# Layer 1's products with adj: from all 22 column blocks to the row block's own columns and a listed, gathered rest

## The chip, the cores and the metric

One core of a Trainium2 chip runs the whole program. The metric is the device time of one execution in microseconds (us). Five runs of the kernel before took 1628.26 to 1630.18 us, with a median of 1629.69 us. The engines are named as in the profile: PE (matmul; PEld loads its weights), DVE (vector), ACT (scalar), POOL (GpSimd) and SP (here only a queue that issues transfers).

## The reference, cut to what matters

A graph of N = 2708 nodes with D = 256 features; `adj` is a 2708 x 2708 matrix in which an off-diagonal element is non-zero with probability 0.00295, and the diagonal is full.

```python
# layer 0
x = _layernorm(x + relu(concat([x, adj @ x], axis=1) @ weight + bias))
# layer 1
R = adj + eye(N);  R = R / R.sum(-1)
Xf = Xa = x
for n in range(2):
    A = _top_p_attention(Xa, W1, W2, W3)   # softmax, cut to the top 0.9 of each row's mass
    Xf = R @ Xf
    Xa = A @ Xa
    Z = Z + Xf @ U1[n].T + Xa @ U2[n].T
x = _layernorm(x + layernorm(x + Z) * ln_g + ln_b)
```

So `adj` is multiplied three times: once in layer 0 and twice in layer 1 (`R @ Xf`, then R times that).

## The kernel before, in words

Everything is float32. The nodes are cut into NB = 22 blocks of 128 rows (the last has 20). The host passes `adj` already transposed and blocked: `adj_d[m, p, k, i]` is the element of row `m*128+i` and column `k*128+p`, so that `adj_d[m, :, k, :]` is directly the weight operand of a matmul. The order of the instructions on each engine's queue is the order of the source (a manual schedule); the semaphores are put in by the framework, and a tile of a pool waits until all readers of the tile that had its room are done.

Layer 0 (L265 to L293) goes over m. `adj_product` (L192) adds 22 products of 128 x 128 by 128 x 257 in PSUM. Its operand comes in two halves, tiles of the pool `adjp` with three rooms, loaded by SP one block ahead (`adj_load`, L187). Two more matmuls add x's own share (L275), then DVE and ACT do the bias, the relu and the layernorm (L282 to L290), and PE turns x1's previous block (L257) and every fourth time projects queries and keys (L242, L247).

Layer 1's first attention step (L537 to L576): logits (L305), top-p by extraction (`extract1`, `finish1`), then for each block t a loop over six groups g: PE transposes four blocks of the masked weights (`turn`, L326), ACT copies them out of PSUM (L329), PE multiplies the group before (`products`, L341). `u1_project` (L427) makes `v` = x U1[0] and `yf` = x U1[1]; `u1_add` (L435) adds row-sum-scaled yf to v. `step1_out` gives the second step its input, ya, its queries and keys, and writes `za` to DRAM.

Layer 1's second step (L766 to L828) goes over periods `per` from -1 to 22, each with six slots g. In a period DVE finishes the top-p search of block `per` (`round_dve` L647, `finish2` L664 to L703, some 105 instructions), ACT does half-rounds of block per+1 and exps of block per+2, PE multiplies block per-1 and computes the logits of per+2. Between these PE does the products with adj: `r_units(n)` (L480) takes n units, a unit being one product of 128 x 128 by 128 x 256 (L197, two matmul records each). A row block takes 22 units, and there are two passes: s = 0 with `yf`, whose result goes into `v` (L511), and s = 1 with `v`, whose result goes to the outputs (L515). The table `units` (L761) says how many units a period takes: 24 before period 0, 84 in period 0, 31 in each of periods 1 to 10 and 49 or 50 in each of 11 to 21. In all 968 units. At the start of each slot 0 the units come before `turn` and before the logits of block per+2, and DVE's `shift` (L610) of those logits comes before or inside its first round.

A block is finished when both its second R product and its attention have arrived (`arrive`, L518); up to two finished blocks at a time then go through `Final` (L708): two layernorms on DVE with their square roots on ACT, spread over the slots, and the store. `za` and `x1b` come back from DRAM for this (L505, L717).

At the end a count of flags (L830 to L837) decides whether `general_path` computes layer 1 again in a slower way; with these inputs it does not run.

Of the kernel before, what the change touches and what calls it, by code (L numbers as in the profile page):

```python
# [8 lines left out]
FP = mybir.dt.float32  # L9
I32 = mybir.dt.int32  # L10
# [9 lines left out]
P = 128  # L20
# [5 lines left out]
ROUNDS = 5  # L26
V0, VSPAN = 0.9375, 88.0
TIE_EPS = 1.5e-5
TOP_S = 0.8999


def chunks(N):
    return [(a, min(N, a + CH)) for a in range(0, N, CH)]
# [6 lines left out]
@with_exitstack  # L40
def gnn_two_layer_kernel(ctx: ExitStack, tc: tile.TileContext, N, xT_d, x_d, adj_d, w0_d, b0_d,
                         w1_d, w2_d, w3_d, u1_d, u2_d, g_d, b_d, out_d):

    nc = tc.nc
    D = x_d.shape[1]
    DA = w1_d.shape[1]
    NB = (N + P - 1) // P
    DC = D // P
    assert N % 2 == 0 and NB % 2 == 0 and N * 2.0 ** -15 < 0.09 and DC == 2 and DA == 64
    assert SEG * (NS - 1) + 8 <= N <= SEG * NS
    CHS = chunks(N)
    KH = NB // 2

    def rows(t):
        return min(P, N - t * P)

    const = ctx.enter_context(tc.tile_pool(name="const", bufs=1))
    dram = ctx.enter_context(tc.tile_pool(name="dram", bufs=1, space=DRAM))
    ctx.enter_context(tc.manual_schedule())

    c = Common()
    c.N, c.D, c.DA, c.NB, c.DC, c.KH, c.CHS, c.rows = N, D, DA, NB, DC, KH, CHS, rows
    c.adj_d, c.out_d = adj_d, out_d  # L80
    c.x1_d = dram.tile([N, D], FP, name="x1_d")
    c.x1b_d = dram.tile([N, D], FP, name="x1b_d")
    c.za_d = dram.tile([N, D], FP, name="za_d")
    c.spill = dram.tile([N, 2 * D], FP, name="spill")


    c.ident = const.tile([P, P], FP, name="ident")
    c.eps = const.tile([P, 1], FP, name="eps")
    c.w1 = const.tile([P, DC, DA], FP, name="w1")
    c.w3 = const.tile([P, DC, DA], FP, name="w3")  # L90
    c.w2 = const.tile([DA, DA], FP, name="w2")
    c.u1 = const.tile([P, DC, 2, D], FP, name="u1")
    c.u2 = const.tile([P, DC, 2, D], FP, name="u2")
    c.gb = const.tile([P, 2, D], FP, name="gb")
    c.rinv = const.tile([P, NB], FP, name="rinv")
    NF = 5 * NB
    flags = const.tile([P, NF], FP, name="flags")
    fint = const.tile([1, 1], I32, name="fint")

    fast = ExitStack()  # L100
    with fast:
        fast_path(fast, tc, c, flags, fint, xT_d, x_d, w0_d, b0_d, w1_d, w2_d, w3_d, u1_d, u2_d, g_d, b_d)
    again = nc.values_load(fint[0:1, 0:1], min_val=0, max_val=P * NF,
                           skip_runtime_bounds_check_because="a count of 0/1 flags")
    with tc.If(again > 0):
        with ExitStack() as gen:
            general_path(gen, tc, c)
# [17 lines left out]
def fast_path(ctx, tc, c, flags, fint, xT_d, x_d, w0_d, b0_d, w1_d, w2_d, w3_d, u1_d, u2_d, g_d, b_d):  # L125
# [2 lines left out]
    ident = c.ident  # L128
    adj_d, out_d, x1_d, za_d = c.adj_d, c.out_d, c.x1_d, c.za_d
    NW = SEG * NS  # L130

    big = ctx.enter_context(tc.tile_pool(name="big", bufs=1))
    adjp = ctx.enter_context(tc.tile_pool(name="adjp", bufs=3))
# [21 lines left out]

    w0 = es[0][:, :2 * DC * D].rearrange("p (c e) -> p c e", e=D)
    b0 = es[1][:, :D]
    nc.scalar.dma_start(out=w0, in_=w0_d.rearrange("(c p) e -> p c e", p=P))

    xT = big.tile([P, DC, N], FP, tag="Y", name="xT")  # L160
# [28 lines left out]
        nc.sync.dma_start(out=a, in_=adj_d[m, :, h * KH:(h + 1) * KH, :])  # L189
        adj_of.setdefault(m, []).append(a)  # L190

    def adj_product(acc, m, y, n, stop, k0=0, k1=NB):  # L192
        p = rows(m)
        halves = adj_of[m]
        for k in range(k0, k1):
            kw = rows(k)
            nc.tensor.matmul(acc[:p, :n], lhsT=halves[k // KH][:kw, k % KH, :p], rhs=y[:kw, k, :n],  # L197
                             start=k == 0, stop=stop and k == NB - 1)
        if k1 == NB:
            adj_of.pop(m)  # L200


    adj_load(0, 0)
# [19 lines left out]


    wqq = small.tile([P, DC, 2, DA], FP, tag="wqq", name="wqq", bufs=1)
    w1n = small.tile([DA, DC, P], FP, tag="w1n", name="w1n", bufs=1)
    for j in range(DC):
        tr = ps_tr()
        nc.tensor.transpose(tr[:DA, 0, :], c.w1[:, j, :], ident)
# [32 lines left out]
        qk_project(0, a, b, lambda j: x1T[:, j, a:b])  # L262

    CB = CH // P
    for m in range(NB):  # L265
        p = rows(m)
        xt = work.tile([P, D], FP, tag="in", name="xt", bufs=3)
        nc.scalar.dma_start(out=xt[:p], in_=x_d[m * P:m * P + p, :])
        acc = ps_acc()
        adj_product(acc, m, y0, D + 1, False)  # L270
        if m + 1 < NB:
            adj_load(m + 1, 0)
            adj_load(m + 1, 1)
        for j in range(DC):
            nc.tensor.matmul(acc[:p, :D], lhsT=xT[:, j, m * P:m * P + p], rhs=w0[:, j, :],  # L275
                             start=False, stop=j == DC - 1)
        if m:
            x1_transpose(m - 1)
        if m >= CB and m % CB == 0:
            x1_qk(m // CB - 1)  # L280
        h = work.tile([P, D], FP, tag="mid", name="h")
        nc.vector.tensor_add(h[:p], acc[:p, :D], b0[:p])  # L282
        nc.vector.scalar_tensor_tensor(h[:p], h[:p], 0.0, xt[:p], op0=ALU.max, op1=ALU.add)
        nc.vector.tensor_scalar(rinv[:p, m:m + 1], acc[:p, D:D + 1], 1.0, None, op0=ALU.add)
        mv, sd = ln_stats(nc, small, c.eps, h, p)
        nc.vector.reciprocal(rinv[:p, m:m + 1], rinv[:p, m:m + 1])
        ln_apply(nc, x1[:p, m, :], h, p, mv, sd)
        nc.sync.dma_start(out=x1_d[m * P:m * P + p, :], in_=x1[:p, m, :])
        xb = work.tile([P, D], FP, tag="x1b", name="xb")
        nc.vector.tensor_add(xb[:p], x1[:p, m, :], c.gb[:p, 1, :])  # L290
        nc.sync.dma_start(out=c.x1b_d[m * P:m * P + p, :], in_=xb[:p])
    x1_transpose(NB - 1)
    x1_qk(len(CHS) - 1)  # L293

# [128 lines left out]
    def u1_project(t):  # L423
        p = rows(t)
        pz = ps_acc()
        for j in range(DC):
            nc.tensor.matmul(pz[:p], lhsT=x1T[:, j, t * P:t * P + p],  # L427
                             rhs=c.u1[:, j].rearrange("p s e -> p (s e)"), start=j == 0, stop=j == DC - 1)
        nc.scalar.copy(v[:p, t, :], pz[:p, :D])
        nc.scalar.copy(yf[:p, t, :], pz[:p, D:])  # L430

    def u1_add(t):

# [34 lines left out]

    r_queue = [(s, m) for s in range(2) for m in range(NB)]
    r_now = []  # L470
    arrived, loads, held = {}, {}, {}
    later = []
    ready = []

    def run_later():
        now, later[:] = later[:], []
        for f in now:
            f()

    def r_units(n):  # L480
        for _ in range(n):
            s, m = r_queue[0]
            y = (yf, v)[s]
            if not r_now:
                r_now[:] = [ps_misc(), 0]
            acc, k = r_now
            if k in (0, KH) and len(r_queue) > 1:
                adj_load(r_queue[1][1], k // KH)
            adj_product(acc, m, y, D, True, k, k + 1)
            r_now[1] += 1  # L490
            if k + 1 == NB:
                r_now.clear()
                r_queue.pop(0)
                base = za_load(m) if s else None
                later.append(lambda s=s, m=m, acc=acc, base=base: r_out(s, m, acc, base))

# [11 lines left out]
    def r_out(s, m, acc, base):  # L508
        p = rows(m)
        if s == 0:  # L510
            nc.vector.scalar_tensor_tensor(v[:p, m, :], acc[:p, :D], rinv[:p, m:m + 1], v[:p, m, :],  # L511
                                           op0=ALU.mult, op1=ALU.add)
        else:
            tmp = work.tile([P, D], FP, tag="mid", name="rtmp")
            nc.vector.tensor_add(tmp[:p], acc[:p, :D], v[:p, m, :])  # L515
            arrive(m, base, tmp, rinv[:p, m:m + 1])
# [31 lines left out]
            ra = finish1(0)  # L548
    for t in range(n_u, NB):
        u1_project(t)  # L550
    adj_load(0, 0)
    adj_load(0, 1)
    ends = None
    for t in range(NB):
        acc = ps_acc()
# [2 lines left out]
        for g in range(NG):  # L558
# [5 lines left out]
            if part and g in (3, 4):  # L564
                part(g - 3)
            products(1)
            if g == 2:
                u1_add(t)
                if t + 3 < NB:
                    extract1(t + 3)  # L570
        ends = step1_out(t, acc, ra)
        ra = ra_next
    products(0)
    for f in ends:
        f()
        r_units(2)  # L576

# [178 lines left out]
    accs = {}  # L758


    units = {-1: 24, 0: 84}  # L761
    units.update({p: 31 for p in range(1, 11)})
    rest = NB * len(r_queue) - (r_now[1] if r_now else 0) - sum(units.values())
    units.update({11 + i: rest * (i + 1) // (NB - 11) - rest * i // (NB - 11) for i in range(NB - 11)})
    assert min(units.values()) > 20
    for per in range(-1, NB + 1):  # L766
        n_r = units.get(per, 0)
        b_act = blocks.get(per + 1) if per >= 0 else None
# [60 lines left out]

    nc.vector.tensor_scalar(flags[:, 2 * NB:3 * NB], bulk[:, 0, :], 1.0e30, None, op0=ALU.is_ge)  # L830
    nc.vector.tensor_scalar(flags[:, 3 * NB:4 * NB], bulk[:, 1, :], 0.0, None, op0=ALU.is_le)
    nc.vector.tensor_tensor(flags[:, 4 * NB:], bulk[:, 3, :], bulk[:, 2, :], op=ALU.is_ge)
    nc.vector.tensor_reduce(fcol, flags, AX.X, ALU.add)
    products(0)
    pf = ps_misc()
# [371 lines left out]
```

## Time and profile before

| | |
|---|---|
| median of 5 runs | 1629.69 us |
| the profiled execution | 1629.63 us |
| its span, first to last instruction | 1627.8 us |
| mean granted PE clock | 0.98 |
| busy: PE, DVE, ACT, POOL | 1557.5, 1125.0, 862.1, 1.5 us |
| layer 0 | 0 to 299 us |
| first step, until its last product | 299 to 777 us |
| second step, DVE's searches | 810 to 1595 us |
| the end | 1595 to 1628 us |

The span is measured from the first to the last instruction, and the execution's time lies 1.8 us above it. Idle time of an engine that is not the bottleneck costs nothing, so each stage has to be read by itself. Every transfer in this kernel is issued by the SP or the ACT queue; the table of queues has no row for POOL. The loads of adj's halves (704 KB each) are 132 issues, 66 blocks times two: a block for each of 22 row blocks in each of the three products.

### The profile page before, as it was taken

To read this page: it belongs to the slowest core of one execution; us is meant where nothing else is said; L and a number is where in the kernel's file an instruction comes from. 1 tells how busy PE (TensorE), PEld (TensorE's weight loads), DVE (VectorE), ACT (ScalarE), POOL (GpSimd) and SP (SyncE) were. 2 spreads that over 40 slices of the span, in tenths; PEclk is the share of its full clock that TensorE was granted. 3 is DMA by queue.
4 is the path that set the end of the run, shared out by engine and by line. 5 is a ranking of instruction groups with operands and counts; after the bars stand their busy time and mean duration, and the time that the engine had idled before them with its cause. 6 is when DMAs were issued, how large, how long until landed. Compare 5 with 4: busy or idle time off the path is not lost.

```text
span 1627.8 us, 20569 instructions
## 1 busy us (share of the span) xinstructions
PE 1557.5 (96%) x7008; PEld 1124.4 (69%) x7008; DVE 1125.0 (69%) x3950; ACT 862.1 (53%) x1470; POOL 1.5 (0%) x18
## 2 busy tenths in 40 slices
PE   8999999789999999999989999999999999999994
PEld 6877777336666666667666776777767777777862
DVE  1212212366777777771199999999988999999995
ACT  1000000345555555553348887887867777777710
POOL 0000000000000000000000000000000000000000
PEclk9999999899999999999999999999999999999997
DMA  5454454100000000000232222221232334333321
GB/s 195 150 160 144 142 162 148 44 0 4 7 7 7 7 7 10 8 7 13 88 107 66 73 78 75 69 79 61 81 96 85 116 108 137 104 109 119 115 77 34
DMA packets 50624, 126.16 MB, mean 78 GB/s; under 512 B 6042, under 2 KB 32334, under 8 KB 50510
## 3 DMA queue, kind: packets, MB, share of 16 engines
q1 hardware_dynamic: 44784, 119.87, 23.0%
q10 hardware_dynamic: 5726, 4.89, 1.1%
q8 instruction: 57, 0.93, 0.2%
q14 instruction: 57, 0.47, 0.1%
HBM read 111.01 MB, written 13.73 MB: 77 GB/s over the span
## 4 chain that ended last, share of the span: by engine, by line
PE 62%; DVE 33%; DMA 2%; issue 1%; ACT 1%; SPq 0%; DVEq 0%; ACTq 0%
PE acc L341 19%; PE acc L197 13%; PE misc L197 9%; DVE w L647 6%; PE lg L305 6%; DVE w L695 5%; PE tr L326 5%; DVE e L698 3%; DVE cand L669 3%; DVE w L664 3%; PE misc L459 3%; PE acc L427 2%; DVE spare L356 2%; DVE srt L354 2%; PE acc L275 1%
## 5 line engine op out<-in xcount | busy, mean ns | idle before, releaser
L329 ACT COPY wT<-tr 128x512 f32<-128x512 f32 (+2 forms) x264 | 136.0, 515 | 315.8 <-PE tr L326 312.8
L197 PE MATMUL misc<-yf,adj_t 128*128 128x256 f32 (+1 forms) x968 | 237.8, 393 | 5.5 <-DVE v L511 5.5
L341 PE MATMUL acc<-ya,wT 128*128 128x256 f32 (+1 forms) x968 | 242.6, 390 | 0.0
L341 PE MATMUL acc<-x,wT 128*128 128x256 f32 (+1 forms) x968 | 240.6, 387 | 0.0
L197 PE MATMUL misc<-v,adj_t 128*128 128x256 f32 (+1 forms) x968 | 228.6, 386 | 0.0
L341 PEld LDWEIGHTS acc<-x,wT 128*128 128x128 f32 (+1 forms) x968 | 169.1, 185 | 80.9 <-issue 46.4
L197 PEld LDWEIGHTS misc<-yf,adj_t 128*128 128x128 f32 (+1 forms) x968 | 175.0, 189 | 67.8 <-issue 37.1
L197 PE MATMUL acc<-y,adj_t 128*128 128x257 f32 (+1 forms) x968 | 218.7, 382 | 0.0
L341 PEld LDWEIGHTS acc<-ya,wT 128*128 128x128 f32 (+1 forms) x968 | 176.7, 187 | 52.6 <-ACT wT L329 14.5
L197 PEld LDWEIGHTS misc<-v,adj_t 128*128 128x128 f32 (+1 forms) x968 | 173.7, 186 | 49.9 <-issue 22.9
L197 PEld LDWEIGHTS acc<-y,adj_t 128*128 128x128 f32 (+1 forms) x968 | 175.7, 185 | 40.0 <-issue 11.5
L326 PE MATMUL tr<-ident,e 128*128 128x128 f32 (+1 forms) x968 | 151.4, 275 | 21.8 <-DVE e L698 21.8
L630 ACT ACTIVATE w<-e,st 128x2708 f32<-128x2708 f32 (+1 forms) x63 | 166.6, 2644 | 0.6 <-ACT e L613 0.6
L632 ACT ACTIVATE w<-e,st 128x2708 f32<-128x2708 f32 (+1 forms) x63 | 166.3, 2639 | 0.0
L305 PE MATMUL lg<-k,q 64*128 64x512 f32 (+3 forms) x528 | 151.8, 603 | 13.7 <-ACT e L312 13.7
L326 PEld LDWEIGHTS tr<-ident,e 128*128 128x128 f32 (+1 forms) x968 | 115.4, 140 | 67.8 <-issue 47.8
L347 DVE MAX8 cand<-e 128x8 f32<-128x170 f32 (+1 forms) x352 | 89.6, 321 | 80.2 <-ACT e L312 80.2
L647 DVE SCALAR_TENSOR_TENSOR w<-e,st 128x2720 f32<-128x2720 f32 (+1 forms) x47 | 143.4, 3051 | 1.7
L282 DVE TENSOR_TENSOR h<-acc,e 128x256 f32<-128x256 f32 (+1 forms) x22 | 9.3, 424 | 185.8 <-PE acc L275 185.8
L258 ACT COPY x1T<-tr 128x256 f32<-128x256 f32 (+1 forms) x22 | 8.0, 364 | 201.3 <-PE tr L257 201.3
L695 DVE MATCH_REPLACE8 w<-eq,w 128x178 f32<-128x178 f32 (+1 forms) x352 | 110.7, 327 | 0.0
L669 DVE MAX8 cand<-w 128x8 f32<-128x170 f32 (+1 forms) x352 | 87.3, 320 | 0.8
(153 smaller groups left out, 1581.7 us busy)
## 6 DMA issues: line engine op xcount, KB each, us to landing
adj_t<-in_adj SPq DMA_DIRECT2D x132, 704.0 KB, 4.2
base<-za_d SPq DMA_DIRECT2D x41, 128.0 KB, 3.3
xt<-in_x ACTq DMA_DIRECT2D x21, 128.0 KB, 2.1
x_d<-x SPq DMA_DIRECT2D x21, 128.0 KB, 1.7
x1b_d<-xb SPq DMA_DIRECT2D x21, 128.0 KB, 2.1
za_d<-za SPq DMA_DIRECT2D x21, 128.0 KB, 1.7
x1b<-x1b_d SPq DMA_DIRECT2D x21, 128.0 KB, 4.9
out<-o SPq DMA_DIRECT2D x21, 128.0 KB, 1.7
```

What stands on the lines that cost most here:

```text
L197: nc.tensor.matmul(acc[:p, :n], lhsT=halves[k // KH][:kw, k % KH, :p], rhs=y[:kw, k, :n], start=k == 0, stop=stop and k == NB - 1)
L305: nc.tensor.matmul(lg[:p, h, :b - a], lhsT=q[o, t * P:t * P + p], rhs=keys[s][o, i, :b - a], start=True, stop=True)
L326: nc.tensor.transpose(tr[:kw, k % 4, :p], e[:p, k * P:k * P + kw], ident[:p, :p])
L329: nc.scalar.copy(wT[:, :full, :p], tr[:, :full, :p])
L341: nc.tensor.matmul(acc[:p, :D], lhsT=wT[:kw, k % 4, :p], rhs=y[:kw, k, :], start=k == 0, stop=k == NB - 1)
L347: nc.vector.max(dst[:p, i * 8:(i + 1) * 8], src[:p, i * step:i * step + w])
L459: nc.tensor.matmul(pz[:p], lhsT=xaT[:, j, :p], rhs=c.u2[:, j].rearrange("p s e -> p (s e)"), start=j == 0, stop=j == DC - 1)
L630: nc.scalar.activation(scr[:b.p, :N], e, AF.Relu, bias=b.nz, scale=b.sq, accum_out=b.relu)
L632: nc.scalar.activation(scr[:b.p, :N], e, AF.Sign, bias=b.nz, scale=b.sq, accum_out=b.sign)
L647: nc.vector.scalar_tensor_tensor(w[:b.p, :, :SEG], e3(b.t)[:b.p], b.d, e3(b.t)[:b.p], op0=ALU.is_ge, op1=ALU.mult, accum_out=b.m)
L669: nc.vector.max(cv[:p, i, :], w[:p, i, :SEG])
L695: nc.vector.match_replace(w[:p, i, :], eq[:p, i * 8:(i + 1) * 8], w[:p, i, :], 0.0)
```

## The change

Layer 1's two R passes no longer multiply all 22 column blocks. Three things are new.

*Lists.* In layer 0, while the halves of adj's row block m are in SBUF, DVE reduces each `[128, 11, 128]` half over i to "has this column an element among the 128 rows" (`name_columns`) and writes a name, a number that grows with nothing but position, for each such column outside the block's own. `Lists` turns the names of three column blocks at a time onto one partition (PE, ACT), takes the largest 160 of the 384 names by 20 rounds of max and match_replace (DVE), raises a flag if one is left, and makes row numbers of them. The first list covers m < 16; its rounds run beside blocks 16 to 21. The second covers the other six; its rounds run in the first ten blocks of the first step, two in each. POOL writes the numbers to DRAM and reads them back as `ix`, 126 x 9 numbers for each m (7 segments of 162, the last two of each being empty).

*adj, gathered.* In the first step, in slot 3 of block t, POOL issues nine indirect transfers that gather 126 rows of 512 bytes each out of adj_d (`adj_gather`), and rebases ix by one small POOL instruction. Two blocks later SP stores the tile to DRAM (`adj_store`).

*The products.* `r_load(s, m)` loads the gathered adj of m, its own diagonal block, and by nine more indirect transfers on POOL (126 rows of 1 KB) the matching rows of yf or v, which are therefore also stored to DRAM. The matching rows go into `yg`, two buffers in turn, in the room that yf had. A row block takes CC + 1 = 10 units instead of 22, and `r_load` of m+1 is issued when m starts. `units` becomes 20 per period: s = 0 in periods 0 to 10, none in -1 and 11, s = 1 in 12 to 22. The six units among `ends` before the second step are gone too, as are the R passes' `adj_load`s. `u1_add` runs two blocks at a time in the first 11 blocks instead of one in each of 22.

```diff
-    def adj_product(acc, m, y, n, stop, k0=0, k1=NB):
+    def adj_product(acc, m, y, n, stop):
...
+    def name_columns(m):
+        for h in range(2):
+            nc.vector.tensor_reduce(some[:, h * KH:(h + 1) * KH], adj_of[m][h], AX.X, ALU.max,
+                                    apply_absolute_value=True)
+        nc.vector.tensor_scalar(some, some, 0.0, None, op0=ALU.not_equal)
+        for a, b, o in ((0, m, 0), (m + 1, NB, -1)):
+            if a < b:
+                nc.vector.scalar_tensor_tensor(names[:, m, a + o:b + o], ramp[:, a:b], -float(m * P * NB),
+                                               some[:, a:b], op0=ALU.add, op1=ALU.mult)
+    class Lists:
...
+        def turn(self):
...
+            for j in range(3):
+                nc.tensor.transpose(tr[:n, j, :], parts[:, :, j], ident)
+            nc.scalar.copy(self.row[:n].rearrange("q (j p) -> q j p", j=3), tr[:n, :3, :])
+            nc.vector.memset(self.top[:n, CAP:], 0.0)
+        def take(self, i0, i1):
+            n = self.n
+            for i in range(i0, i1):
+                t8 = self.top[:n, 8 * i:8 * i + 8]
+                nc.vector.max(t8, self.row[:n])
+                nc.vector.match_replace(self.row[:n], t8, self.row[:n], 0.0)
+        def end(self):
...
+            nc.gpsimd.dma_start(out=flat.rearrange("(r k) -> r k", k=CPAD), in_=self.int[:n])
+            nc.gpsimd.dma_start(out=ix[:CW, a:b, :], in_=c.list_d[a:b].rearrange("m p c -> p m c"))
+    def adj_gather(m):
+        a = adjp.tile([P, KH, P], FP, tag="adj", name="adj_t")
+        for i in range(CC):
+            nc.gpsimd.indirect_dma_start(out=a[:CW, i, :], out_offset=None, in_=adj_rows,
+                                         in_offset=bass.IndirectOffsetOnAxis(ap=ix[:CW, m, i:i + 1], axis=0))
+        nc.gpsimd.tensor_scalar(ix[:CW, m, :], ix[:CW, m, :], m * P * NB, P * NB - 1, op0=ALU.subtract, op1=ALU.min)
+        staged[m] = a
+    def adj_store(m):
+        nc.sync.dma_start(out=c.adjc_d[m], in_=staged.pop(m)[:CW, :CC, :].rearrange("p c i -> p (c i)"))
...
+        name_columns(m)
         adj_product(acc, m, y0, D + 1, False)
...
+        if m == ML:
+            lists.turn()
...
+        if m >= ML:
+            i = m - ML
+            lists.take(CAP // 8 * i // (NB - ML), CAP // 8 * (i + 1) // (NB - ML))
+    lists.end()
...
+        nc.sync.dma_start(out=c.yf_d[:p, t, :], in_=yf[:p, t, :])
...
+    def r_load(s, m):
+        a = adjp.tile([P, KH, P], FP, tag="adj", name="adj_t")
+        nc.sync.dma_start(out=a[:CW, :CC, :].rearrange("p c i -> p (c i)"), in_=c.adjc_d[m])
+        nc.sync.dma_start(out=a[:rows(m), CC, :], in_=adj_d[m, :rows(m), m, :])
+        y = yg[:, m % 2]
+        rows_d = (c.yf_d, c.v_d)[s].rearrange("p k d -> (p k) d")
+        for i in range(CC):
+            nc.gpsimd.indirect_dma_start(out=y[:CW, i, :], out_offset=None, in_=rows_d,
+                                         in_offset=bass.IndirectOffsetOnAxis(ap=ix[:CW, m, i:i + 1], axis=0))
+        if s == 0:
+            nc.sync.dma_start(out=y[:rows(m), CC, :], in_=c.yf_d[:rows(m), m, :])
+        r_in[s, m] = a, y
...
             if not r_now:
                 r_now[:] = [ps_misc(), 0]
+                if m + 1 < NB:
+                    r_load(s, m + 1)
             acc, k = r_now
-            if k in (0, KH) and len(r_queue) > 1:
-                adj_load(r_queue[1][1], k // KH)
-            adj_product(acc, m, y, D, True, k, k + 1)
+            a, y = r_in[s, m]
+            kw = CW if k < CC else p
+            rhs = v[:p, m, :] if s and k == CC else y[:kw, k, :]
+            nc.tensor.matmul(acc[:p, :D], lhsT=a[:kw, k, :p], rhs=rhs, start=k == 0, stop=k == CC)
...
+            nc.sync.dma_start(out=c.v_d[:p, m, :], in_=v[:p, m, :])
+            if m == NB - 1:
+                r_load(1, 0)
...
             products(1)
+            if g == 0 and t > 1:
+                adj_store(t - 2)
             if g == 2:
-                u1_add(t)
+                for k in range(2 * t, min(NB, 2 * t + 2)):
+                    u1_add(k)
...
+                if t < 10:
+                    lists.take(2 * t, 2 * t + 2)
+                if t == 9:
+                    lists.end()
+            if g == 3:
+                adj_gather(t)
...
+    for m in sorted(staged):
+        adj_store(m)
+    yg = big.tile([P, 2, CC + 1, D], FP, tag="Y", name="yg")
+    r_load(0, 0)
     for f in ends:
         f()
-        r_units(2)
...
-    units = {-1: 24, 0: 84}
-    units.update({p: 31 for p in range(1, 11)})
...
+    each = NB * (CC + 1)
+    units = {p: each * (p + 1) // 11 - each * p // 11 for p in range(11)}
+    units.update({p: each * (p - 11) // 11 - each * (p - 12) // 11 for p in range(12, 23)})
```

## The prediction

> **What bounds the kernel now.** I read the engine rows and the chain's shares first, then the chain in order of time, then busy time by stretch, then the timeline where the second step starts.
>
> ```profile
> PE 1557.5 (96%) x7008; PEld 1124.4 (69%) x7008; DVE 1125.0 (69%) x3950; ACT 862.1 (53%) x1470; POOL 1.5 (0%) x18
> ...
> PE 62%; DVE 33%; DMA 2%; issue 1%; ACT 1%; SPq 0%; DVEq 0%; ACTq 0%
> ```
>
> PE is busy 96% of the span, yet the chain of waits is DVE's for a third. Where, the chain in order of time shows (start, length; not consecutive lines):
>
> ```profile
> 523.56 1.93 PE acc L341 x8
> 542.73 1.93 PE acc L341 x8
> ...
> 881.12 2.99 DVE e L698
> ...
> 912.70 2.99 DVE e L698
> ...
> 1226.78 3.65 PE misc L197 x16
> ...
> 1282.14 2.99 DVE e L698
> ...
> 1320.65 2.99 DVE e L698
> ```
>
> The first step runs in blocks of 542.73 - 523.56 = 19.17 us and is PE's. In the second step the last instruction of DVE's search, L698, comes every 31.6 us early (912.70 - 881.12) and every 38.5 us late (1320.65 - 1282.14). Now DVE's busy time in both parts (length, busy, granted clock, DMA share, GB/s):
>
> ```profile
> 853.50:1106.80 253.30, 243.58 (x835) 0.99 0.23 74
> 1106.80:1595.00 488.20, 450.25 (x1527) 0.99 0.31 99
> ```
>
> Early, DVE is busy 243.58/253.30 = 96.2% and every piece of the chain is its own: it is the bound, and R units there fill holes of PE. Late it is still busy 92.2%, since the two layernorms per finished block add about 7 us per period; PE is busy 476.85 of 488.20 us there. So late both engines are full, and this is the reading that decides: PE may lose much, and DVE stands right behind it.
>
> **What the change removes.** Units: 968 before, 2 x 22 x 10 = 440 after, so 528 fewer. A unit is two records, and 16 records take 3.65 us (L197 above), 0.456 us each: 528 x 0.456 = 241 us of PE work. I count only what DVE lets through.
>
> (a) *Late periods.* If DVE ran at its early 96.2%, its 450.25 us would take 468.2 us instead of 488.2: **-20.0 us**. In the early ones PE's units fall from 31 to 20 per period, and nothing is gained.
>
> (b) *Start of the second step.* The timeline:
>
> ```profile
> 799.82 8.23 PE L197 MATMUL misc<-yf,adj_t 128*128 128x256 f32 x36
> ...
> 807.98 1.13 PE L305 MATMUL lg<-k,q 64*128 64x512 f32 x4
> ...
> 809.81 3.05 DVE L647 SCALAR_TENSOR_TENSOR w<-e,st 128x2720 f32<-128x2720 f32 x1
> ```
>
> DVE's first round waits for `shift`, shift for the logits L305, and these for 18 units in front of them on PE's queue. Three units remain there (1.4 us): -6.9 us. The six units between `ends` cover ACT's copies only in part; from their gaps (0.3, 0.4 and 1.1 us between when ACT was done and PE went on) I take -1.8. Sum **-8.7 us**, if the gathered rows of m = 0 are there by 799.
>
> (c) *The end.* Period 22 had no units and now has 20. Its PE work, 1595 to 1611.5, has no hole; three units precede the wait for DVE's last mask, 17 follow it: 17 x 0.456 = **+7.7 us**. Against it one block instead of two is left for the last round of layernorms: DVE's second copy of L734 to L736 and the statistics, **-1.5 us**.
>
> **What it adds.** (d) *Layer 0*, PE bound, 11.03 us a block. `name_columns`: a reduce of 1408 elements; MAX8 of 170 takes 0.32 us, L647 of 2720 takes 3.05, so 1.07 ns an element and 1.65 us each, 3.6 with the small ones. A round of max and match_replace over 384: 2 x 0.55 us; 3.4 rounds in each of blocks 16 to 21, 3.7 us. With the 2.9 us from L282 to L290 that makes 10.2 of 11.03 us: hidden behind PE, 0.8 us from not being. Halves of adj are released later (DVE reads them too), at 7 us into a block instead of 5.5; a load takes 4.2 us and is needed at 16.5. The three transposes of the first list stand in PE's queue: **+0.9 us** (0.31 each). Those of the second fit into PE's wait for x1's last block (296.9 to 299.1), and its rounds on DVE end at 305.2 where the first MAX8 of the extraction starts at 305.45. The two POOL transfers of zeros stand before y0's column of ones, needed at 31.7 us; they have some 25 us.
>
> (e) *First step.* DVE per block: 14.24 of 19.20 us busy, plus two rounds (2.2) and a second `u1_add` (0.47): 16.9, hidden under PE's 19.17; without that cover 2.7 us for each of ten blocks. SP issues one store of 567 KB per block more, and 22 stores of yf before; in the second step a load of adj, its diagonal, in the first pass also yf's own rows, and a store of v, per row block, for the two halves before. Each issue takes 0.3 to 0.4 us; that is under 2 us per row block of 15.8, and no wait on SP gets a later releaser than the product before.
>
> (f) *The gathers.* POOL gets 198 of them in the first step and 396 in the second; before it did 1.5 us of work in all, and no row shows one. From below: a plain issue on SP takes 0.35 us (L464, 0.30 to 0.32; L189, 0.38). From above: issue to landing of 128 rows of 1 KB:
>
> ```profile
> za_d<-za SPq DMA_DIRECT2D x21, 128.0 KB, 1.7
> x1b<-x1b_d SPq DMA_DIRECT2D x21, 128.0 KB, 4.9
> ```
>
> Between 0.35 and 4.9 us lies a factor of 14; I take the middle in ratio, g = 1.3 us. First step: 9 x 1.3 + 1.7 to land + 0.3 = 13.7 of 19.17 us; the limit is g = 1.9. Behind a late gather SP waits in `adj_store`, behind it the `za` stores, behind these DVE's L463. Second step: two row blocks per period, so 18 g against 31.6 us; the limit is g = 1.75. Behind a late gather PE waits in slot 0, behind it the logits, behind these DVE. Cost at 1.3: nothing.
>
> (g) *DVE beside POOL.* Whether a gather holds DVE up is not shown either. Bounds per gather: nothing, or its whole 1.3 us; a gain is excluded, as POOL takes over no DVE work. L647 takes 3.040 to 3.053 us under all the traffic of 47 instances; this spread, 0.013 us, is the nearest row: 396 x 0.013 = **+5.1 us**.
>
> Sum: -20.0 - 8.7 + 7.7 - 1.5 + 0.9 + 5.1 = -16.5 on the profiled 1629.63, so **1613 us**. The profiled execution lies 0.06 us from the median, and nothing is to be corrected.
>
> Two rules speak against the change. The Trainium skill, SBUF — State Buffer, section "Who interferes with whom", says that a DVE instruction with two SBUF inputs and a GpSimd instruction that reads SBUF exclude each other for the whole instruction; no run here shows it, and by it (g) would go towards rival C's time. DMA: Bandwidth & Descriptors, section "Anatomy of one DMA", gives a transfer from GpSimd a fixed cost of about 2 us, mostly until completion is confirmed; if all of it held POOL, an estimate from that page would be B's 1680, and if it only delays landing, the sum stays.
>
> **The rivals.** *B, POOL's queue is the bound.* From g = 1.75 the gathers set the early periods' length, 18 g; with 11 of them, the 16.5 us are gone at g = 1.83. At g = 2.0 the first step's blocks take 20.0 us (22 x 0.83 = +18) and the early periods 36 (11 x 4.4 = +48): 1613 + 66 = **1679 us**; at 2.5, over 1900. For it: nine small issues in a row where the profile has none; against: the page's issues of 0.3 to 0.4 us.
>
> *C, the gathers slow DVE down.* Of 31.6 us some 20 are instructions with two inputs in SBUF (four at 3.05, L698, 16 of 0.33 at L695), 65%; POOL would be busy 18 x 1.3/31.6 = 74%. If a gather holds such an instruction back for a third of g, 0.43 x 0.65 = 0.28 us: 396 x 0.28 = 111 on 1608, **1719 us**. It decides from 21.6/396 = 0.055 us on. For it: DVE has no slack anywhere in the second step, so every hold counts; against: the same instruction never varied under 126 MB of traffic.
>
> *D, nothing to gain.* The stretch 1286.0 to 1324.5, with little waiting for PE, has DVE at 36.36/38.5 = 94.4%: square roots on ACT and base rows from DRAM come in between. At that share (a) is 488.2 - 477 = 11; if m = 0 also arrives late, (b) is nothing: -11 + 7.7 - 1.5 + 0.9 + 5.1 = +1, **1631 us**.
>
> *E*, that a list overflows and `general_path` runs: a column has an element among 128 rows with 1 - 0.99705^128 = 31.5%, so 121 of 384 and a spread of 9.1; 160 lies 4.3 spreads above. Against 1%, then over 1300 us more.
>
> **How the numbers follow.** Chances: forecast 0.48, B 0.20, C 0.20, D 0.10, E and the rest 0.02. The forecast's own range is 1603 (g without (g), and DVE at 97%) to 1622 (the late share of D). Over all, 1602 to 1720: below lies little, above it the far ends of B and C, some 0.17. What can be told from no change is 0.2%, 3.3 us. Faster: 0.46 from the forecast and 0.03 from D. Same: 0.02 and 0.04. Slower: B, C, 0.03 of D and E.
>
> **What would show it.** POOL's rows with gathers: mean below 1.7 us, and L647 still at 3.05 (else C); L698 every 31.5 us until period 11 and every 37 to 38 after (else B, with PE waiting for a transfer at the products of r_units); first L647 about 801; last L698 about 1568 (1592 - 28.7 + 5.1), the end some 42 us behind it (35.8 now, + 7.7 - 1.5). I am wrong if PE's chain hides something that DVE's busy time doesn't show, above all if periods lengthen where DVE idles.

## The result: slightly slower, and the profile after

The changed kernel takes 1634.08 us (median of 23 runs, 1630.51 to 1636.94), the kernel before 1629.91 us in the same sets (44 runs): a ratio of 1.0025, 95% interval 1.0019 to 1.0030. The forecast was 1613 us, so its sign was wrong. In the profiled executions (1636.03 us after, 2 us above its median; 1629.63 us before) PE lost 177 us of work and the span grew by 6.5 us. The forecast had PE lose 241 us: the matmuls that are left take longer (the logits 682 ns on average instead of 603) at a mean granted clock of 0.904 instead of 0.98.

The page after, cut to the rows that answer to those shown of before and to the gathers (engines; queues; the costliest groups; transfers with KB each and us from issue to landing):

```profile
PE 1380.4 (84%) x5958; PEld 965.8 (59%) x5958; DVE 1246.0 (76%) x4186; ACT 861.3 (53%) x1474; POOL 781.1 (48%) x642
...
q0 software_dynamic: 35104, 64.37, 17.0%
...
L590 POOL DMA_INDIRECT yg<-v_d,ix x198 | 261.5, 1321 | 190.8 <-PE misc L608 108.0
L590 POOL DMA_INDIRECT yg<-yf_d,ix x198 | 284.1, 1435 | 77.1 <-issue 43.7
...
L285 POOL DMA_INDIRECT adj_t<-in_adj,ix x198 | 221.8, 1120 | 161.6 <-DMA adjc_d<-adj_t 96.6
...
L780 DVE SCALAR_TENSOR_TENSOR w<-e,st 128x2720 f32<-128x2720 f32 (+1 forms) x47 | 143.8, 3060 | 1.7
...
adj_t<-in_adj,ix POOLq DMA_INDIRECT x198, 2.7
yg<-yf_d,ix POOLq DMA_INDIRECT x198, 4.6
yg<-v_d,ix POOLq DMA_INDIRECT x198, 5.4
```

The unknown prices have rows now: a gather holds POOL for 1.12 to 1.44 us, and DVE's long instruction beside them takes 3.060 us on average, where the kernel before has 3.051 (its L647). POOL is no bound, but only just. In the second pass most of its idle time is waiting for PE's products (108.0 of 190.8 us). In the first pass its gathers stand almost back to back: 1.435 us each and some 0.3 us idle behind each make 1.74 us, and a period of 31.84 us has 18 of them, 1.77 us each. Yet from block 0 to block 8 DVE is busy 245.23 of 254.74 us, 96.3% (96.2% before), so POOL does not set the pace there either. So neither POOL's queue nor contention with DVE explains the time.

Where it went is read by stage. A block is timed by the start of the last instruction of DVE's search (L698 before, L831 after; its "end" below); the late stage goes from that of block 8 to that of block 21. DVE's busy time there, before (length, busy, granted clock, DMA share, GB/s):

```profile
1103.10:1592.02 488.92, 450.91 (x1531) 0.99 0.32 101
```

and after:

```profile
1099.00:1593.86 494.86, 450.15 (x1537) 0.82 0.46 114
```

The same DVE work, the forecast's 450 us, takes 5.9 us *more*, not 20 us less: DVE's share fell from 92.2% to 91.0%. PE's share there fell too, from 98% to 71% (478.54 of 488.92 us, 351.74 of 494.86), so DVE hardly waits for PE. The list of DVE's waits in that stretch, after (what waited, for what: total us, times, longest), has two rows:

```profile
DVE h L648 <- issue: 15.6, 6, 3.7
DVE h L648 <- DMA base<-za_d: 10.3, 4, 3.4
```

and before, among several others, this one for the same row:

```profile
DVE h L525 <- DMA base<-za_d: 2.9, 5, 1.0
```

After the change all 25.9 us stand before one instruction, L648, which adds the base row of a finished row block; the "issue" rows are the same wait where no releaser was found. The timeline around one of them (after):

```profile
1410.53 0.33 SPq L656 DMA_DIRECT2D za_d<-h  x1
...
1410.91 0.42 SPq L625 DMA_DIRECT2D base<-za_d  x1
...
1412.32 0.41 DVE L638 TENSOR_TENSOR rtmp<-misc,v 128x256 f32<-128x256 f32 x1
...
1415.26 0.48 DVE L648 SCALAR_TENSOR_TENSOR h<-rtmp,rinv,base 128x256 f32<-128x256 f32 x1 [2.53 <-DMA base<-za_d]
```

SP issues the load of `base` behind a store that itself waits for DVE (L656). DVE wants the row 1.8 us later (1412.73) and gets it 4.35 us after the issue. The kernel before has the same order and the same 1.8 us:

```profile
1339.83 0.33 SPq L533 DMA_DIRECT2D za_d<-h  x1
...
1340.20 0.43 SPq L505 DMA_DIRECT2D base<-za_d  x1
...
1341.62 0.40 DVE L515 TENSOR_TENSOR rtmp<-misc,v 128x256 f32<-128x256 f32 x1
...
1342.48 0.48 DVE L525 SCALAR_TENSOR_TENSOR h<-rtmp,rinv,base 128x256 f32<-128x256 f32 x1 [0.46 <-DMA base<-za_d]
```

but there it comes after 2.28 us, and DVE waits 0.46 us. This is no single case: in all ten waits after the change the row is wanted 1.8 us after its load's issue and comes after 3.9 to 5.5 us (median 4.1). Before, there are five such waits, four of them with the row there after 2.2 to 2.4 us. The number doubled because with 20 units per period one of a period's two row blocks always ends at this place. The whole account of the span against before: second step begins 5.3 us earlier (end of block 0 at 844.3 instead of 849.6), blocks 0 to 8 +1.2, blocks 8 to 13 -7.0, blocks 13 to 21 +13.0, the end (from the last L831) +4.6 us: +6.5.

The theory to test: the gain is there, and late base rows eat it, because the load is issued late *and* lands slowly beside the gathers. The rivals: the gain was never there (D); or the gathers hold DVE up in some other way (C).

### The profile page after: what moved, and what is told of

Read it like the earlier page. It is cut to its first block, busy times and chain, and to the rows that moved or that the text cites. A ratio compares the mean times of both kernels' runs of the same rounds, so it can differ in the third digit from the quotient of the medians.

```text
span 1634.3 us, 20062 instructions
## 1 busy us (share of the span) xinstructions
PE 1380.4 (84%) x5958; PEld 965.8 (59%) x5958; DVE 1246.0 (76%) x4186; ACT 861.3 (53%) x1474; POOL 781.1 (48%) x642
## 5 line engine op out<-in xcount | busy, mean ns | idle before, releaser
L590 POOL DMA_INDIRECT yg<-v_d,ix x198 | 261.5, 1321 | 190.8 <-PE misc L608 108.0
L590 POOL DMA_INDIRECT yg<-yf_d,ix x198 | 284.1, 1435 | 77.1 <-issue 43.7
L427 PE MATMUL tr<-ident,e 128*128 128x128 f32 (+1 forms) x968 | 164.4, 293 | 170.2 <-DVE e L831 170.2
L285 POOL DMA_INDIRECT adj_t<-in_adj,ix x198 | 221.8, 1120 | 161.6 <-DMA adjc_d<-adj_t 96.6
L442 PE MATMUL acc<-ya,wT 128*128 128x256 f32 (+1 forms) x968 | 258.3, 408 | 1.6 <-ACT wT L430 1.6
L427 PEld LDWEIGHTS tr<-ident,e 128*128 128x128 f32 (+1 forms) x968 | 122.9, 149 | 222.0 <-issue 197.0
L608 PE MATMUL misc<-yg,adj_t 126*128 126x256 f32 (+2 forms) x836 | 226.5, 413 | 30.1 <-DMA adj_t<-adjc_d 27.2
L442 PEld LDWEIGHTS acc<-ya,wT 128*128 128x128 f32 (+1 forms) x968 | 187.3, 199 | 73.9 <-issue 40.5
L608 PEld LDWEIGHTS misc<-yg,adj_t 126*128 126x128 f32 (+2 forms) x836 | 158.8, 202 | 87.4 <-issue 32.7
L406 PE MATMUL lg<-k,q 64*128 64x512 f32 (+3 forms) x528 | 172.5, 682 | 26.9 <-ACT e L413 13.7
L780 DVE SCALAR_TENSOR_TENSOR w<-e,st 128x2720 f32<-128x2720 f32 (+1 forms) x47 | 143.8, 3060 | 1.7
```

What stands on the lines that cost most here:

```text
L285: nc.gpsimd.indirect_dma_start(out=a[:CW, i, :], out_offset=None, in_=adj_rows, in_offset=bass.IndirectOffsetOnAxis(ap=ix[:CW, m, i:i + 1] ...
L406: nc.tensor.matmul(lg[:p, h, :b - a], lhsT=q[o, t * P:t * P + p], rhs=keys[s][o, i, :b - a], start=True, stop=True)
L427: nc.tensor.transpose(tr[:kw, k % 4, :p], e[:p, k * P:k * P + kw], ident[:p, :p])
L442: nc.tensor.matmul(acc[:p, :D], lhsT=wT[:kw, k % 4, :p], rhs=y[:kw, k, :], start=k == 0, stop=k == NB - 1)
L590: nc.gpsimd.indirect_dma_start(out=y[:CW, i, :], out_offset=None, in_=rows_d, in_offset=bass.IndirectOffsetOnAxis(ap=ix[:CW, m, i:i + 1], ...
L608: nc.tensor.matmul(acc[:p, :D], lhsT=a[:kw, k, :p], rhs=rhs, start=k == 0, stop=k == CC)
```

## The experiments

Each result is given as the median time, its ratio to the kernel before in the same set of runs, and the 95% interval of that ratio.

### The first four edits, which all came out slow together

*Base early.* The base row is loaded at its row block's first unit (row block 20 excepted, where the kernel's order of the two arrivals stays):

```diff
                 if m + 1 < NB:
                     r_load(s, m + 1)
+                if s and m != 20:
+                    r_base[m] = za_load(m)
...
-                base = za_load(m) if s else None
+                base = (r_base.pop(m) if m in r_base else za_load(m)) if s else None
```

> The changed kernel, with the load of a row block's base row (za_d) for the second R pass issued at the block's first unit instead of its last (all but m = 20). In the changed kernel DVE waits once in each late period, ten waits of 2.1 to 3.7 us in the instruction that needs this row, 25.9 us in all. Theory 1 (order: the last unit falls in slot 2 of every period, so the load is queued on SP right behind the store that waits for DVE's arrive of slot 1) and theory 2 (traffic: the gathers make the load land late) both expect those waits gone: late periods of 37.5 to 38 us instead of 40.2, the kernel some 18 to 24 us faster than the changed one, about 1610 to 1616 us, ratio to before 0.988 to 0.992. If DVE idles for another reason (PE's lower clock, an ACT result), the period stays at 40 and the time above 1628.

Measured: 1659.36 us, 1.0187 [1.0164, 1.0210].

*Without the row gathers.* In `r_load`:

```diff
-        for i in range(CC):
+        for i in range(CC if s == 0 and m < 2 else 0):
```

> The changed kernel without the 378 gathers of yf and v rows in the second step, except those of m = 0 and 1 of the first pass; the products read what stands in the buffers, so the R passes are not computed. Theory 1 (order on SP) expects the waits for the base row to stay near 2 us each and the time near 1628 or above; theory 2 (traffic) expects the base row to land in about 2.7 us as before the change, the waits below 1 us, and a gain of 12 us or more, about 1622 or less. If gathers hold DVE's instructions, early periods fall from 31.84 to 31.69 us and the mean of the long two-input instruction from 3060 to 3052 ns; this is worth 1 to 3 us.

Measured: 1629.86 us, 1.0015 [0.9999, 1.0032].

*Dummies before the second step*, so that PE is not idle between the logits:

```diff
+    def warm(n):
+        d = ps_misc()
+        for _ in range(n):
+            nc.tensor.matmul(d[:, :D], lhsT=ident, rhs=v[:, 0, :], start=True, stop=True)
...
-                    r_units(n_r // (2 * NL))
+                    warm(3)
```

(and `warm(2)` in each of `ends`.)

> The changed kernel with 24 products of 128 x 128 by 128 x 256 that nobody reads put between the last blocks of the first step and into the start of the second (two behind each of the three end stages, three behind each of the six logits), where units of R stood before the change. Theory 3: at the start of the second step PE's granted clock falls since the units went, the logits take 2.07 instead of 1.13 us, and DVE's first round starts at 805.1 instead of 801. Expected: logits 1.13 us, first round at 801 to 802, 3 to 4 us faster than the changed kernel, ratio to before about 1.000. If the clock is not it, the filler costs time: 1634 or above.

Measured: 1681.52 us, 1.0339 [1.0324, 1.0353].

*No units in period 22:*

```diff
-    units.update({p: each * (p - 11) // 11 - each * (p - 12) // 11 for p in range(12, 23)})
+    units.update({p: 22 for p in range(12, 22)})
```

> The changed kernel with the second R pass spread over periods 12 to 21, 22 units each, instead of 12 to 22, 20 each: period 22 has none. Expected from the end: 17 units of PE less behind DVE's last mask, so 40.4 us from DVE's last subtraction to the end become about 36 to 37, 4 us less. Row blocks now end in changing slots. Theory 1 then expects fewer waits for the base row, some 10 us less in all, 1620 us; theory 2 expects them unchanged or longer, since the gathers come closer together, 1630 us.

Measured: 1676.53 us, 1.0289 [1.0273, 1.0306].

The first, third and fourth lie more than 40 us above what was expected. The second, by its time, stands beside theory 1, but its base waits are 6.4 us in all and not some 2 us each, which is theory 2's sign. One thing is common to all four: block 0 of the second step ended at 857 to 865 us, though the first and the fourth change no instruction before it. The kernel before took its usual 1628.8 us in the same set; the unedited changed kernel was not in it. So something besides the edits was at work, and no size could be read from these runs. The next set was built to find out what.

### Is it the edit, the build or the chip?

The changed kernel unedited:

> The changed kernel again, unedited, on the chip of this set of runs. In the four runs so far the first search block of the second step ended at 857 to 865 us, not at 844.3 as in the changed kernel's profile, although two of the four edits touch nothing before it. Theory L (how a build lies in memory, or something else that goes with the build): this kernel stands at 1634 again, its first block ends at 844 to 846, DVE has no stalls over 0.8 us other than those for the base row. Theory C (the chip or the set of runs): it stands at 1650 to 1665, its first block ends near 860, and the stalls of 1 to 5 us with no releaser are there too.

Measured: 1633.92 us, 1.0022 [1.0012, 1.0031]; block 0 ends at 845.0 us.

One instruction more (`nc.vector.tensor_reduce(fcol, flags, AX.X, ALU.add)` twice):

> The changed kernel with one instruction more: DVE's last reduction of the flags, after the second step, is made twice (0.1 us by itself). Theory L: some 1650 to 1675 us, first block of the second step later than 850 us, though the instructions up to there are the same. Theory C: the same as the unedited kernel of this set within 0.3%.

Measured: 1635.53 us, 1.0035 [1.0021, 1.0049], 0.1% from the unedited one. Theory L's 1650 to 1675 did not come; the next run settles it.

The very kernel that had taken 1659 us:

> The base row's load early again (as in the run before), beside the unedited kernel. Theory C: faster than the unedited kernel of this set by the base waits, 10 to 20 us less. Theory L: 1655 to 1665, with the unedited kernel at 1634.

Measured: **1611.93 us**, 0.9890 [0.9873, 0.9906]. Same file, 47 us less than in the first set. So it is not the build, and theory C (the chip or the set of runs) holds for the disturbance; more on it in the last section. Of the edit itself this shows that an early base row brings 22.0 us (1633.92 - 1611.93) and turns the change into a gain of 1.1%. DVE's busy time in the same stretch as above, now:

```profile
1099.94:1569.89 469.95, 449.99 (x1536) 0.84 0.48 119
```

The same 450 us in 470 instead of 495: a share of 95.75%, where the forecast had 96.2%. A period of blocks 13 to 21 takes 37.8 us instead of 40.4; the forecast had 37 to 38.

### Late place or slow landing?

Base early and no row gathers:

> Base row early, and the second step's row gathers left out (with those of 20 of the first step's 22 row blocks: yg keeps old rows, so the rest of layer 1's products is made of wrong rows). Of the run without the gathers alone (1629.9) the base waits left 6.8 us in the trace. If the gathers' traffic makes both the base waits and the stalls without a releaser: 1618 to 1628, late periods 37.5 to 38.5 us, no DVE gap over 0.8 us up to the last block. If the stalls do not come from the gathers: 1635 or more.

Measured: 1609.08 us, 0.9870 [0.9854, 0.9887], below the 1618 to 1628 expected; the pauses of the first set did not come here.

Late place, no row gathers, now undisturbed:

> The changed kernel, base row at its late place, without the second step's row gathers (and without those of 20 of the first step's 22 row blocks: layer 1's products are made of old rows). If the slow landing beside the gathers makes the wait: base waits of 5 to 8 us instead of 25.9, late periods 38.2 to 38.5 us, 1612 to 1617. If the late place alone makes it: 1628 to 1634, late periods 40.

Measured: 1616.97 us, 0.9933 [0.9917, 0.9950]. DVE's waits between 1099 and 1574.6 us:

```profile
DVE h L648 <- DVE rtmp L638: 2.7, 5, 1.0
DVE h L648 <- DMA base<-za_d: 2.7, 4, 1.3
DVE h L648 <- issue: 1.9, 1, 1.9
```

7.3 us instead of 25.9, all still before L648 and still ten. The timeline around one of them:

```profile
1403.71 0.42 SPq L625 DMA_DIRECT2D base<-za_d  x1
...
1405.12 0.41 DVE L638 TENSOR_TENSOR rtmp<-misc,v 128x256 f32<-128x256 f32 x1
...
1405.96 0.48 DVE L648 SCALAR_TENSOR_TENSOR h<-rtmp,rinv,base 128x256 f32<-128x256 f32 x1 [0.43 <-DMA base<-za_d]
```

The same place and the same 1.8 us, but the row is there after 2.25 us. In the ten waits it is 2.2 to 3.7 us (median 2.3), where beside the gathers it was 3.9 to 5.5.

Gathers and all, the load four units before the row block's last (`if k == CC - 4 and s and m != 20`, and nothing at the first unit):

> The changed kernel, gathers and all, with the base row loaded four units before the row block's last (a slot, some 6 us, earlier) and not at its first unit. Landing takes 4 to 5.5 us, so a lead of 6 + 1.8 us covers it: 1611 to 1614, as with the load at the first unit. If the queue holds that load up by itself (other loads in front of it): 1618 or more.

Measured: 1611.53 us, 0.9896 [0.9880, 0.9913]; no wait for a base row is left before the last period. A lead of some 6 us does as much as one of a whole row block.

Put together (us):

| | base late | base early |
|---|---|---|
| with the row gathers | 1633.92 | 1611.93 |
| without | 1616.97 | 1609.08 |

The gathers cost 17.0 us where the base row is late, and 2.9 us where it is early. So most of what they cost comes through one small load that lands slowly beside them, and not through POOL's, PE's or DVE's own instructions. Both parts are needed: the place alone, without gathers, costs 7.9 us. The 1616.97 us stand in another set and on another chip than the other three times, and each time is known to some 2.7 us; by the ratios to the kernel before, the 17.0 become 14.5 and the 7.9 become 10.3. The traces say the same: DVE's waits for the row fall by 18.6 us without the gathers, and 7.3 us are left.

The control, the kernel *before* with its base row early (at the first of its 22 units):

> The kernel before with the base row's load at its row block's first unit (but for row block 20), as in the changed kernel with that edit. Theory W (the forecast's gain was there, and only the late base row took it back): the trace of before shows 5.1 us of base waits, in periods that PE fills, so at most 3 us come back: 1625 to 1630. Theory S (the early load by itself is the gain, and the listed products bring nothing): 1611 to 1618, like the changed kernel with the early load.

Measured: 1626.14 us, 0.9979 [0.9969, 0.9988]. The early load alone brings 3.4 us there, at the edge of what was expected. With it on both sides, listing and gathering brings 1626.14 - 1611.93 = 14.2 us (two sets again; by the ratios 14.5); the forecast said 16.5.

### The start and the end, on top of the early base row

These runs and the one with the base row early alone (1611.93 us), from which their gains are taken, stand in different sets on different chips. A difference of 3 or 4 us between them is hardly more than the noise; the times of the stages in the traces are firmer.

No units in period 22:

> Base row early and period 22's 17 units given to periods 12 to 21. If the units at the end cost what the tail grew by: 4 to 6 us less than with the base row early alone (1611.9), so 1606 to 1608. If the tail is bound by the last block's own chain: 1611 to 1613. On a chip like that of the first set: some 1655, and the first block of the second step later than 855 us.

Measured: 1608.87 us, 0.9873 [0.9856, 0.9889]: 3.1 us less, not 4 to 6. The end shrinks from 39.2 to 31.7 us, that is 7.5; but blocks 0 to 21 take 730.7 instead of 724.8 us: in them DVE is busy 2.7 us more (698.0 and 695.3), with work that the end had before, and idle 3.3 us more.

Dummies before the second step:

> Base row early, and 24 products of identity x a row block, that nobody reads, in period -1, where the kernel before has its R units. If PE's low granted clock cost the start 4 us (logits of 2.07 us where full clock takes 1.13): first block's end at 841 us and 1607 to 1610. If the dummies stand in the way of the logits as the R units did: first block's end at 848 to 850, 1615 to 1617.

Measured: 1607.72 us, 0.9868 [0.9851, 0.9884]: 4.2 us less. Busy time of PE around the start (length, busy, granted clock, DMA share, GB/s), in the changed kernel:

```profile
750.00:800.00 50.00, 42.28 (x174) 0.83 0.64 136
```

and with the dummies:

```profile
750.00:800.00 50.00, 49.72 (x232) 1.00 0.65 137
```

A product of logits in the timeline, in the changed kernel:

```profile
787.67 2.07 PE L406 MATMUL lg<-k,q 64*128 64x512 f32 x4 [1.31 <-ACT e L746]
```

and with the dummies:

```profile
789.61 1.12 PE L406 MATMUL lg<-k,q 64*128 64x512 f32 x4
```

With nothing between them PE waits for ACT, its granted clock is 0.83 instead of 1.00 in this stretch, and five of the first six products of logits take some 2.07 us instead of 1.12. With the matmuls that nobody reads, DVE's first round starts at 803.1 us instead of the 806.0 of the run with the base row early alone.

All three edits together, twice, in two sets:

> Base row early, no units in period 22, dummies in period -1. The sum of the two runs before it, if they are independent: 1602 to 1606 where both help, 1611 to 1613 where the dummies cost what the tail saves.

> Early base row, no units at the end, dummies in period -1, again: 1604 where the first block of the second step ends at 842 us. If the stalls without a releaser of the first set return (there the early base row alone took 1659 and not 1612): 1640 to 1655, in the other two runs of this set as well.

Measured: **1604.31 us**, 0.9849 [0.9832, 0.9865], and 1605.29 us, 0.9857 [0.9841, 0.9874]. Within the noise the gains add up (3.1 + 4.2 = 7.3 expected, 7.6 and 6.6 found). This is the fastest version found, 1.5% below the kernel before.

## Why the prediction was wrong, point by point

**(a) Late periods, -20.0 forecast: this step failed.** "If DVE ran at its early 96.2%" takes DVE's share from periods in which no row block of the second pass ends, and carries it over to periods in which two do. Each brings an instruction that needs a row from a transfer. In before's trace the wait for it was small (2.9 us), and I took it as gone with PE's waits; (e) even says that no wait on SP gets a later releaser. But the price of a wait for a transfer is not its length in the trace of before: it is the landing time less the slack, and the change made the landing time longer (2.28 us, then 4.35 us, in the two timelines) and the waits twice as many (ten, not five). They came to 25.9 us, and the stretch gave +5.9 us. The prediction's own sign of being wrong, periods that lengthen where DVE idles, is what came. With the row loaded early the stretch gives 488.92 - 469.95 = -19.0 us, so the reading that DVE stands right behind PE was right. Its size was nearly right too, but not all of it comes from PE's units: in the kernel before with its base row early the stretch takes 485.0 us, and against that 15.0 us are left.

**(b) Start, -8.7 forecast.** DVE's first round started 4.7 us earlier, block 0 ended 5.3 us earlier. The units in front of the logits were gone as said; not foreseen was what their absence does to PE's clock. With the dummies the first round is 6.7 us earlier (809.8 to 803.1); 801 was forecast, and the last 2 us stay unexplained.

**(c) The end, +7.7 - 1.5.** The end grew by 4.6 us, from 35.8 to 40.4. The 17 units in it are worth 7.5 us, as the run without them shows; the rest of the end became shorter by more than the 1.5 I counted. What I did not see is that moving them into the periods costs most of it again.

**(d), (e) Layer 0 and the first step.** Hidden as forecast: PE's last product of the first step ends at 777.0 us (777.3 before).

**(f) The gathers.** Taken: 1.3 us, between 0.35 and 4.9. Found: 1.12, 1.44 and 1.32 us in the three groups, below both limits (1.9 and 1.75). The middle in ratio between far bounds came out well, with some luck: POOL also stands idle for 0.3 us behind a gather, which the sum does not have, and with that the 1.44 become 1.74, just under the limit. What was missing is the other side of the same transfers: they occupy the 16 DMA engines for 17.0% of the span, and a load that I did not look at lands later beside them. Where it is held up is not shown. Rival B falls, narrowly.

**(g) DVE beside POOL, +5.1 forecast.** Too much: L780 takes 0.009 us more than L647 (3.060 and 3.051), 0.4 us over its 47 instances, and a period of blocks 0 to 8 takes 31.84 us instead of 31.69, 1.2 us over eight; without the row gathers 0.7 of these are still there (254.23 us from block 0 to block 8, where the kernel before takes 253.49). The whole cost of the row gathers, with base early, is 2.9 us. Rival C falls. The Trainium skill, SBUF — State Buffer, section "Who interferes with whom", says that a DVE instruction with two SBUF inputs contends with a GpSimd instruction that reads SBUF, that the contention is an exclusive lock, and that issue order decides who blocks. In this trace one does hold the other up, and the loser is POOL (timeline after):

```profile
1284.72 3.05 DVE L797 SCALAR_TENSOR_TENSOR w<-e,st 128x2720 f32<-128x2720 f32 x1
1284.95 3.70 POOL L590 DMA_INDIRECT yg<-v_d,ix  x1 [0.30 <-PE misc L608]
...
1288.95 0.99 POOL L590 DMA_INDIRECT yg<-v_d,ix  x1 [0.30 <-issue]
```

The gather that starts inside DVE's instruction ends 0.88 us after it; the next, free one takes 0.99 us. Of the 594 gathers 74 take over 2 us, and every one of these starts inside one of DVE's instructions of some 3 us. The other way round nothing shows: ten of DVE's instructions on `w` (L780 and the like) start while a gather runs, and they take 3.050 us on average, no more than the others. Whether the gather still read SBUF then, the trace does not tell. I read the rule as a price on DVE; here it is a price on POOL, and POOL had just room for it.

**The rivals.** D, at 1631, came nearest, and it named "base rows from DRAM" among what comes between DVE's instructions. But its cause was a share of 94.4% that DVE would keep, and a late first row block. The measured late share was lower (91.0%), from a wait that grew, and with that wait gone 95.75% was reached: the gain was there. So D's time was met by another mechanism, which is luck. E did not happen: `general_path` would have cost over 1300 us. One sum of the prediction is off by a little: with DVE at 97% and without (g), the low end of its range is 1604 us and not 1603.

## What to carry to other kernels

When a change adds transfers, list every load whose landing some engine waits for, with its slack (issue to use), and ask what happens when landing takes twice as long; a wait of 0.46 us in the old trace became one of 2.5 us here, and one of that kind stood in each late period. Loads that are known long ahead belong at the head of their stage: here a few lines brought 22 us, and 3.4 us in the kernel that had no gathers. And look at what remains where filler work is taken away: here PE then waited for ACT, its granted clock was 0.83 instead of 1.00, and most products of logits took nearly twice as long.

## What the runs showed of the hardware that was not expected

The kernels with gathers are not equally fast everywhere. The first four runs stood on one chip, the later eleven on three others. The same file, base early, took 1659.36 us on the first and 1611.93 us on another; the kernel before, 1628.80 and 1629.57 us. In the first set DVE has pauses before instructions for which the trace shows no wait. One instruction's row in the page of the base-early run there,

```profile
L830 DVE MATCH_REPLACE8 w<-eq,w 128x178 f32<-128x178 f32 (+1 forms) x352 | 111.3, 329 | 9.4 <-issue 8.9
```

and in that of the same file on the other chip:

```profile
L830 DVE MATCH_REPLACE8 w<-eq,w 128x178 f32<-128x178 f32 (+1 forms) x352 | 110.7, 327 | 0.0
```

Its work is as long, but 9.4 us of idle time stand before it. Without the row gathers that chip showed no such pause over 0.8 us in DVE's blocks 1 to 21, and the time was 1629.86 us (1616.97 elsewhere), with the first step late. (In the first step the gathers of adj were still there.) So the pauses go with the gathers on that chip. It was used in one set only, so a property of the chip and one of that hour can't be told apart; what makes the pauses stays open. A reader who ships such a kernel should time it on more than one chip.
